# Layer 2 of a graph attention network: columns 256 to 767 of half of a tile's rows summed on TensorE, the first norm's statistics on ScalarE

## The chip, the cores and the metric

The kernel runs on one core of one Trainium2 chip. The metric is device time in microseconds (us), the median of the runs. The core has five engines that run their own instruction streams in order and wait for each other by semaphores: TensorE (PE, with its weight loads as PEld), VectorE (DVE), ScalarE (ACT), GpSimd (POOL) and SyncE (SP, which here only starts transfers).

## The reference

Two graph attention layers over 10000 nodes and 170000 edges (80000 drawn in both directions and a loop on each node; the layer adds a loop of its own), all in float32:

```python
def gat_conv(x, edge_index, W, a_src, a_dst, bias, heads, out_ch, concat):
    src, dst = edge_index with self loops
    xl = (x @ W).reshape(n, heads, out_ch)
    e = leaky_relu(alpha_src[src] + alpha_dst[dst], 0.2)     # alpha_* = einsum of xl with a_*
    e = exp(e - segment_max(e, dst)[dst])
    alpha = e / (segment_sum(e, dst)[dst] + 1e-16)
    out = segment_sum(xl[src] * alpha, dst) + bias            # heads side by side, or their mean

h  = gat_conv(x, W1, heads=4, out_ch=256)                     # 1024 columns
h1 = relu(layer_norm(h, g1, be1)) + (x @ Wr1 + br1)
h  = gat_conv(h1, W2, heads=1, out_ch=768)                    # 768 columns
out = layernorm(x + layer_norm(h, g2, be2) + (h1 @ Wr2 + br2))
```

The change lies in the last two lines: for every node the weighted sum over its neighbours' rows of 768 numbers, the residual product h1 @ Wr2, the first norm (with g2 and be2) and the second one of the sum with x.

## The kernel before

The first part of the program sorts the nodes by degree into 79 tiles of 128 nodes and makes lists of their neighbours; then comes layer 1, and at its end a table in DRAM holds for each node its row of layer 2: 768 numbers of h1 @ W2, and two logits. Layer 2 (the function `ordered_layer2`) goes over the tiles one after the other. A tile has n rows, n being the largest number of neighbours in it (7 to 41; 17.35 on the mean, 1371 in all). Row k holds the k-th neighbour of each of the 128 nodes, one node on a partition, so that a row is 128 x 770 numbers. Row 0 (the node itself) is loaded by SP, the other 1292 rows come by an indirect DMA each, which POOL issues (`gather`, L473). They go into a ring of 41 places in SBUF: the gather for a row may start once all readers of the row that stood 41 places earlier are done, and POOL issues the gathers in the order of the rows, so a place that comes free late holds up all gathers behind it.

The work of a tile t is spread over two turns of the loop `for t in range(NT)`:

- In turn t-1, at row `turn`, `weights_of(t)` computes the logits of all rows of t (`logits`, L536 to L544: a few small instructions of DVE, and Exp on ACT), for which all gathers of tile t must have landed. Three rows later (`turn + LEAD`) `normalised` divides by their sum, and then `summed` lets ACT write a diagonal matrix of the weights e of each row (L1310) and PE multiply it with columns 512 to 767 of the row (L1311, in fp32 two matmul instructions each). These products of n - n//6 rows add up in PSUM, on the bank that holds the residual's last 256 columns (`big`), together with the bias b2 (L1320).
- At the top of turn t-1 stands `residual(t)`, 16 products of h1 with Wr2 (L1363, 32 instructions), so PE's order is residual, sums, residual, sums.
- In turn t, DVE adds e times the first 512 columns of each row to `acc` in PSUM (`weigh`, L574), and for the last n//6 rows also the columns 512 to 767 onto PE's sums (L1439). At row n//2 SP loads the operand of `residual(t + 2)` (512 KB) and x of the next tile (384 KB).
- After the last row come the statistics of the first norm (L585, L587 on DVE, L589 and L590 on ACT). The rest of the norms follows in turn t+1: at row 3 (LEAD) the first norm and the two additions (L599, L601, L1373, L1374 on DVE), at row 6 the second norm on ACT (L1378 to L1384), at row 9 the scatter of the finished 128 rows to the output on POOL (L1386).

Tiles of 26 rows and more (three of the 79, the last one among them) are parted: their logits and sums are made in two parts, and a factor `fade` brings the first to the second one's maximum. The order in which each engine gets its instructions is the order of this code, written by hand (`manual_schedule`). In the views, `w` are pieces of the old weight buffer w2 that now hold h1, x, the tile being normed and some of the diagonals; `big` is a PSUM tile of two banks.

## Time and profile before

| what | us |
| --- | --- |
| median of 3 runs (lowest to highest) | 5207.22 (5200.71 to 5215.73) |
| the profiled execution | 5214.41 |
| its span | 5212.5 |
| layer 2, first gather to last gather | 3174.05 to 5159.25 |
| PE, DVE, ACT, POOL busy over the span | 4580.7, 4359.7, 3210.2, 3481.6 |
| granted TensorE clock over the span | 0.931 |

The views are of the profiled execution; times are us from the start of the span unless ns is written. In a row of a group, the count is followed by the busy time, the mean ns of one instruction, and the idle time of the engine just before them with what ended it. "issue" is time in which an engine waited for nothing that the profile shows. "remote" is a release that the profile puts down to none of the engines shown. Matmuls are pipelined, so the mean of one is longer than its share of the busy time. A row of the timeline is start, duration, engine, line and what ran, and in brackets the idle time before it.

### The profile page before, as it was taken

The numbers are of one execution on the slowest core, as the hardware profiler recorded it, in microseconds if no ns is written. First come the engines' busy times: TensorE is split into PE (matmuls) and PEld (weight loads), VectorE is DVE, ScalarE is ACT, GpSimd is POOL, SyncE is SP. The second block draws the span as 40 slices with busy tenths as digits, with TensorE's granted clock in tenths as the row PEclk, the third lists the DMA queues.
The fourth block names the chain that finished last, engine by engine and source line by source line (L and its number), as shares of the span: only waits on it lengthen the run. The fifth ranks groups of instructions, "written<-read, shape, count | busy, mean of one in ns | idle before, by whom it ended". The sixth has DMA issues, their size and how long they took to land. (4 is left out here: it accounts for less than half of the span.)

```text
span 5212.5 us, 56646 instructions
## 1 busy us (share of the span) xinstructions
PE 4580.7 (88%) x13332; PEld 2524.8 (48%) x13332; DVE 4359.7 (84%) x7113; ACT 3210.2 (62%) x9002; POOL 3481.6 (67%) x3722
## 2 busy tenths in 40 slices
PE   9999997999999997899999997877887877788876
PEld 4443444554444443444445554554554555555554
DVE  7887877999998988888999985888787878888877
ACT  5744446899998987898999982433333333333333
POOL 6876756666776766676766644767667666666664
PEclk9999998999999998999999998988888888888888
DMA  4333449999999989999999977999899999999995
GB/s 154 122 107 125 109 150 346 347 364 370 381 381 377 382 299 329 346 374 370 375 379 370 359 266 265 333 323 328 312 323 326 329 326 324 325 324 326 323 326 194
DMA packets 433436, 1588.28 MB, mean 305 GB/s; under 512 B 77208, under 2 KB 82136, under 8 KB 433095
## 3 DMA queue, kind: packets, MB, share of 16 engines
q0 software_dynamic: 321040, 1283.72, 68.1%
q1 hardware_dynamic: 99490, 269.38, 14.3%
q10 hardware_dynamic: 12564, 31.47, 1.9%
q8 instruction: 112, 1.84, 0.1%
q14 instruction: 230, 1.88, 0.1%
HBM read 1426.26 MB, written 177.29 MB: 308 GB/s over the span
## 5 line engine op out<-in xcount | busy, mean ns | idle before, releaser
L473 POOL DMA_INDIRECT ring<-table,slots x2663 | 2677.3, 1005 | 1366.0 <-issue 588.7
L563 ACT ACTIVATE ring<-ring,e 128x256 f32<-128x256 f32 x4468 | 1823.9, 502 | 65.3 <-DVE e L981 38.6
L574 DVE SCALAR_TENSOR_TENSOR acc<-ring,e,acc 128x512 f32<-128x512 f32 (+1 forms) x2280 | 1456.9, 639 | 97.4 <-PE acc L936 21.2
L570 DVE TENSOR_TENSOR acc<-acc,ring 128x1024 f32<-128x1024 f32 x869 | 1070.1, 1231 | 81.2 <-ACT ring L563 16.9
L1363 PE MATMUL big<-wr,w 128*128 128x512 f32 (+1 forms) x2464 | 834.9, 495 | 46.2 <-issue 46.0
L1161 PE MATMUL half<-w,hT 128*128 128x512 f32 (+1 forms) x2528 | 843.5, 486 | 4.0 <-issue 3.7
L180 PE MATMUL big<-wr,xT 128*128 128x512 f32 x1896 | 833.9, 596 | 0.5 <-ACT xT L897 0.5
L1311 PE MATMUL big<-ring,diagonals 128*128 128x256 f32 x1706 | 527.7, 449 | 298.6 <-issue 264.1
L1363 PEld LDWEIGHTS big<-wr,w 128*128 128x128 f32 x2464 | 478.6, 194 | 391.8 <-issue 357.7
L1161 PEld LDWEIGHTS half<-w,hT 128*128 128x128 f32 x2528 | 472.5, 189 | 348.4 <-issue 310.3
L1311 PEld LDWEIGHTS big<-ring,diagonals 128*128 128x128 f32 x1706 | 383.9, 227 | 427.4 <-issue 338.3
L180 PEld LDWEIGHTS big<-wr,xT 128*128 128x128 f32 x1896 | 357.2, 192 | 420.8 <-issue 420.0
L936 PE MATMUL acc<-ring,ident 128*128 128x512 f32 x992 | 467.8, 621 | 86.8 <-ACT ring L563 61.3
L544 ACT ACTIVATE e<-e 128x19 f32<-128x19 f32 (+14 forms) x82 | 17.6, 215 | 641.6 <-issue 243.1
L695 ACT ACTIVATE scr<-scr 128x256 f32<-128x256 f32 x624 | 250.5, 403 | 160.6 <-DVE scr L688 153.6
L936 PEld LDWEIGHTS acc<-ring,ident 128*128 128x128 f32 x992 | 190.9, 197 | 326.1 <-issue 195.9
L635 PE MATMUL one<-wr,mixed 128*128 128x512 f32 x702 | 307.6, 592 | 0.0
L1310 ACT ACTIVATE diagonals<-ident,e 128x128 f32<-128x128 f32 x853 | 259.1, 387 | 70.7 <-DVE total L552 20.3
L589 ACT ACTIVATE sd<-mv,eps 128x1 f32<-128x1 f32 x158 | 46.1, 292 | 400.1 <-issue 159.9
L1311 PE MATMUL big<-ring,w 128*128 128x256 f32 x672 | 199.1, 436 | 65.9 <-issue 56.5
L700 POOL TENSOR_TENSOR row<-row,none 128x1024 f32<-128x1024 f32 x69 | 168.2, 2438 | 116.0 <-DVE scr L688 45.1
L635 PE MATMUL one<-w,xT 128*128 128x512 f32 x492 | 228.5, 602 | 9.3 <-DMA w<-in_W_dram 6.4
(246 smaller groups left out, 4809.6 us busy)
## 6 DMA issues: line engine op xcount, KB each, us to landing
ring<-table,slots POOLq DMA_INDIRECT x2663
h_d<-hT SPq DMA_DIRECT2D x79, 512.0 KB
table<-row SPq DMA_DIRECT2D x78, 516.0 KB
w<-h_d SPq DMA_DIRECT2D x77, 512.0 KB
table<-row SPq DMA_DIRECT2D x79, 385.0 KB
ring<-table SPq DMA_DIRECT2D x79, 385.0 KB
w<-x_d SPq DMA_DIRECT2D x79, 384.0 KB
x_d<-xt SPq DMA_DIRECT2D x77, 384.0 KB
```

The source lines that it names most:

```text
L180: nc.tensor.matmul(p[:, c:e], aT[:, j, :], w[:, j, c:e], start=(j == 0), stop=(j == k - 1))
L473: nc.gpsimd.indirect_dma_start(out=to, out_offset=None, in_=table, in_offset=bass.IndirectOffsetOnAxis(ap=index, axis=0), **more)
L563: nc.scalar.activation(row[:, s], row[:, s], AF.Copy, scale=e[:, h:h + 1])
L570: nc.vector.tensor_add(acc[:, :c], acc[:, :c], row[:, :c])
L574: nc.vector.scalar_tensor_tensor(acc[:, s], row[:, s], e[:, h:h + 1], (acc if first is None else first)[:, s], op0=OP.mult, op1=OP.add)
L635: nc.tensor.matmul(p, aT[:, j, :], w[:, j, :], start=(start and j == 0), stop=(j == k - 1), skip_group_check=True)
L695: nc.scalar.activation(m[:, s], m[:, s], AF.Copy, accum_out=row[:, C1 + i * H1 + h:C1 + i * H1 + h + 1])
L936: nc.tensor.matmul(acc[:, c:c + BANK], ident, ring.slot(q + k)[:, c:c + BANK], start=(k == 0), stop=(k == m - 1))
L1161: nc.tensor.matmul(q, hT[:, j, :], w2[:, j, c:c + q.shape[1]], start=(j == 0), stop=(j == K1 - 1))
L1310: nc.scalar.activation(diagonal, ident, AF.Copy, scale=e[:, k - lo, :])
L1311: nc.tensor.matmul(to, diagonal, ring.slot(at + k)[:, ON_PE2:C2], start=False, stop=(k == n - 1 - by_vector(t)), skip_group_check=True)
L1363: nc.tensor.matmul(r[:, c:d], hT[:, j, :], wr2[:, j, c:d], start=(j == 0), stop=(j == K1 - 1 and d < C2), skip_group_check=True)
```

## The change

The split of the sums is turned. For the first half of a tile's rows (`on_pe`; of the first part, where a tile is parted) PE now sums columns 256 to 767 in products of 512 into two PSUM tiles of its own (`accs`), and DVE adds columns 0 to 255 of these rows beside them; for the other half DVE adds all 768 columns on top of PE's sums, and PE has no part in them. ACT instead of PE puts b2 into the accumulator (from the third tile on). ACT copies each residual out of PSUM into SBUF (`held`). The sum and the squares of the first norm are taken on ACT, as they already are in the second norm. The second stage of `norms` comes at row `soon` = min(6, n // 2, n - 4) instead of row 3, behind the logits of the next tile in most turns. Four rows of the second part of each parted tile are summed whole on PE, and the steps of that part come earlier. There are 16 diagonals instead of 28.

```diff
--- before.py
+++ after.py
@@ -50,9 +50,8 @@
 RING1 = 31
 RING2 = 41
 LEAD = 3
-DIAGONALS = 20
-ON_PE2 = 512
-ALL_BY_VECTOR = 6
+DIAGONALS = 8
+ALONE2 = 256
 SHARE = 4
 ON_PE1 = 5
 PARTED2 = 26
@@ -1239,7 +1238,7 @@
         at = [FIRST1[t] + k for t in turns for k in range(SLOTS1[t])]
         with tc.tile_pool(name="b2", bufs=1) as pool, tc.tile_pool(name="small2", bufs=2) as small, \
                 tc.tile_pool(name="ps_acc2", bufs=2, space=PSUM) as ps_acc, \
-                tc.tile_pool(name="ps_q2", bufs=3, space=PSUM) as ps_big, tc.manual_schedule():
+                tc.tile_pool(name="ps_q2", bufs=2, space=PSUM) as ps_big, tc.manual_schedule():
 
...
@@ -1282,19 +1281,16 @@
                 n = SLOTS[t]
                 return [0, n - 8 if t == NT - 1 else n // 2, n] if n >= PARTED2 else [0, n]
 
...
+            def on_pe(t):
+
+                return cuts_of(t)[1] // 2
 
             def parted_at(t):
 
                 lo = cuts_of(t)[1]
-                return ((LEAD + 1, 2 * LEAD + 1) if whole(t) else (lo - LEAD, lo - 1)) if len(cuts_of(t)) > 2 else ()
+                if len(cuts_of(t)) == 2:
+                    return ()
+                return (LEAD + 1, 2 * LEAD + 1) if t == NT - 1 else (lo - 3 * LEAD, lo - 2 * LEAD)
 
             def weights_of(t):
 
@@ -1302,33 +1298,38 @@
                 n, at, cuts = SLOTS[t], FIRST[t], cuts_of(t)
                 ad = small.tile([P, H2], F32, name="ad")
                 nc.vector.tensor_add(ad, ring.slot(at)[:, C2:C2 + H2], lift)
-                to = rs[t][:, C2:2 * C2 - ON_PE2]
-
-                def summed(e, lo, hi, more=None, m=0):
-                    for k in range(lo, hi):
-                        diagonal = next(turning)
-                        nc.scalar.activation(diagonal, ident, AF.Copy, scale=e[:, k - lo, :])
-                        nc.tensor.matmul(to, diagonal, ring.slot(at + k)[:, ON_PE2:C2],
-                                         start=False, stop=(k == n - 1 - by_vector(t)), skip_group_check=True)
-                        if k - lo < m:
-                            nc.tensor.matmul(more, diagonal, ring.slot(at + k)[:, :ON_PE2],
-                                             start=False, stop=(k - lo == m - 1), skip_group_check=True)
-                        if k - lo == m - 1:
-                            nc.scalar.copy(ring.slot(at + lo)[:, :ON_PE2], more)
-
-                def add_b2():
-                    nc.tensor.matmul(to, ident, b2_b[:, ON_PE2:], start=False, stop=False, skip_group_check=True)
+
+                def diagonal_of(e):
+                    diagonal = next(turning)
+                    nc.scalar.activation(diagonal, ident, AF.Copy, scale=e)
+                    return diagonal
+
+                def multiplied(to, a, row, lo, hi, start, stop):
+                    for c in range(lo, hi, BANK):
+                        d = min(hi, c + BANK)
+                        nc.tensor.matmul(to[:, c - lo:d - lo], a, row[:, c:d], start=start, stop=stop,
+                                         skip_group_check=True)
 
                 e, top = logits(small, ring, at, at + cuts[1], ad, H2, C2)
                 yield {0: (e, None, None)}
+                accs[t] = ps_acc.tile([P, 2 * BANK], F32, name="acc")
+                to, m = accs[t][:, BANK:], on_pe(t)
                 if len(cuts) == 2:
                     normalised(small, e, H2, turns[t])
-                    add_b2()
+                    if t < 2:
+                        multiplied(to, ident, b2_b, ALONE2, C2, True, False)
+                    else:
+                        nc.scalar.copy(to, b2_b[:, ALONE2:])
                 else:
                     doubled(e, turns[t])
                     total = small.tile([P, H2], F32, name="total")
                     nc.vector.reduce_sum(total, e.rearrange("p k h -> p h k"), axis=AX.X)
-                summed(e, 0, cuts[1] - by_vector(t))
+                for k in range(m):
+                    multiplied(to, diagonal_of(e[:, k, :]), ring.slot(at + k), ALONE2, C2,
+                               not k and len(cuts) > 2, k == m - 1)
+                held = pool.tile([P, C2], F32, name="held", bufs=2)
+                nc.scalar.copy(held, rs.pop(t)[:, :C2])
+                rs[t] = held
...
-                    nc.scalar.activation(to, to, AF.Copy, scale=fade)
-                    add_b2()
-                    m, more = whole(t), b2_b[:, :ON_PE2]
-                    if m:
-                        more = ps_big.tile([P, 2 * BANK], F32, name="big")[:, :ON_PE2]
-                        nc.tensor.matmul(more, ident, b2_b[:, :ON_PE2], start=True, stop=False, skip_group_check=True)
-                    summed(e, lo, hi, more, m)
-                    yield lo, (e, fade, ring.slot(at + lo)[:, :ON_PE2] if m else more)
+                    more = ps_big.tile([P, 2 * BANK], F32, name="big")
+                    multiplied(more, ident, b2_b, 0, C2, True, False)
+                    for k in range(WHOLE):
+                        multiplied(more, diagonal_of(e[:, k, :]), ring.slot(at + lo + k), 0, C2, False, k == WHOLE - 1)
+                    nc.scalar.copy(ring.slot(at + lo)[:, :C2], more[:, :C2])
+                    yield lo, (e, fade, ring.slot(at + lo)[:, :C2])
 
             def residual(t):
 
@@ -1360,26 +1359,30 @@
                 for c in range(0, C2, BANK):
...
-            def norms(t, h, r, means):
-
-                stats = deviation(small, [a for m in means for a in pieces(m, C2 - ON_PE2)])
+            def mean_and_deviation(spare, a):
+
+                less, inv = (small.tile([P, 1], F32, name=n, bufs=4) for n in ("less", "inv"))
+                nc.scalar.activation(spare, a, AF.Copy, accum_out=less)
+                nc.scalar.activation(less, less, AF.Copy, scale=-1.0 / C2)
+                nc.scalar.activation(spare, a, AF.Square, bias=less, accum_out=inv)
+                nc.scalar.activation(inv, inv, AF.Ln, scale=1.0 / C2, bias=eps)
+                nc.scalar.activation(inv, inv, AF.Exp, scale=-0.5)
+                return less, inv
+
+            def norms(t, h, r, sums):
+
+                less, inv = mean_and_deviation(h, sums)
                 yield
-                scaled(h, means, stats, g2_b, be2_b)
-                nc.vector.tensor_add(h, h, r[:, :C2])
+                nc.vector.scalar_tensor_tensor(h, sums, less, g2_b, op0=OP.add, op1=OP.mult)
+                nc.vector.scalar_tensor_tensor(h, h, inv, be2_b, op0=OP.mult, op1=OP.add)
+                nc.vector.tensor_add(h, h, r)
                 nc.vector.tensor_add(h, h, xs.pop(t))
                 yield
                 o = pool.tile([P, C2], F32, name="out")
-                less, inv = (small.tile([P, 1], F32, name=n) for n in ("less", "inv"))
-                nc.scalar.activation(o, h, AF.Copy, accum_out=less)
-                nc.scalar.activation(less, less, AF.Copy, scale=-1.0 / C2)
-                nc.scalar.activation(o, h, AF.Square, bias=less, accum_out=inv)
-                nc.scalar.activation(inv, inv, AF.Ln, scale=1.0 / C2, bias=eps)
-                nc.scalar.activation(inv, inv, AF.Exp, scale=-0.5)
+                less, inv = mean_and_deviation(o, h)
                 nc.scalar.activation(less, less, AF.Copy, scale=inv)
                 nc.scalar.activation(o, h, AF.Identity, bias=less, scale=inv)
                 yield
@@ -1387,12 +1390,15 @@
                     out=out, out_offset=bass.IndirectOffsetOnAxis(ap=nodes(turns[t]), axis=0),
                     in_=o, in_offset=None, bounds_check=N - 1, oob_is_err=False)
 
...
@@ -1405,39 +1411,36 @@
                     ahead = weights_of(t)
                     ready += itertools.islice(ahead, 2)
                 es, later, cuts = dict(ready[0]), ahead, cuts_of(t)
-                acc = ps_acc.tile([P, BANK], F32, name="acc")
+                sums = accs.pop(t)[:, ALONE2:]
                 if not t:
                     ring.fetch(RING2)
                 next(last, None)
+                soon = min(2 * LEAD, n // 2, n - LEAD - 1)
                 ready, ahead, turn = [], iter(()), n
                 if t + 1 < NT:
 
                     ahead = weights_of(t + 1)
                     turn = min(max(n // 3, cuts[-2] + 1, n + cuts_of(t + 1)[1] + 4 * LEAD - ring.size), n - LEAD)
...
                 for k in range(n):
                     if k in parted_at(t):
                         es.update([e for e in [next(later)] if e])
                     if k in (turn, turn + LEAD):
                         ready += itertools.islice(ahead, 1)
-                    if k in (LEAD, 2 * LEAD, 3 * LEAD):
+                    if k in (soon, soon + LEAD, soon + 2 * LEAD):
                         next(last, None)
                     lo = max(c for c in cuts[:-1] if c <= k)
                     weights, fade, more = es[lo]
                     row = ring.slot(FIRST[t] + k)
                     if k == 0 and len(cuts) > 2:
-                        nc.vector.tensor_scalar(acc[:, :ON_PE2], row[:, :ON_PE2], weights[:, 0], None, op0=OP.mult)
-                    else:
-                        if k == lo and fade is not None:
-                            nc.vector.scalar_tensor_tensor(acc[:, :ON_PE2], acc[:, :ON_PE2], fade, more,
-                                                           op0=OP.mult, op1=OP.add)
-                        if not lo or k - lo >= whole(t):
-                            weigh(acc, row, weights[:, k - lo], ON_PE2, None if k else b2_b)
-                            if k >= n - by_vector(t):
-                                sums = rs[t][:, C2:2 * C2 - ON_PE2]
-                                nc.vector.scalar_tensor_tensor(sums, row[:, ON_PE2:C2], weights[:, k - lo], sums,
-                                                               op0=OP.mult, op1=OP.add)
+                        nc.vector.tensor_scalar(sums[:, :ALONE2], row[:, :ALONE2], weights[:, 0], None, op0=OP.mult)
+                    elif k < on_pe(t):
+                        weigh(sums, row, weights[:, k], ALONE2, None if k else b2_b)
+                    elif lo and k == lo:
+                        nc.vector.scalar_tensor_tensor(sums, sums, fade, more, op0=OP.mult, op1=OP.add)
+                    elif not lo or k - lo >= WHOLE:
+                        weigh(sums, row, weights[:, k - lo], C2)
                     ring.fetch(FIRST[t] + k + 1 + ring.size)
                     if k == n // 2:
                         if t + 2 < NT:
@@ -1449,8 +1452,8 @@
                     pass
                 if not t:
                     nc.vector.tensor_add(be2_b, be2_b, adds[1])
-                    nc.vector.tensor_add(be2_b, be2_b, q[:, :C2])
-                last = norms(t, h, rs[t], [acc, rs[t][:, C2:2 * C2 - ON_PE2]])
+                    nc.vector.tensor_add(be2_b, be2_b, br2_q)
+                last = norms(t, h, rs.pop(t), sums)
             for _ in last:
                 pass
```

DVE, at the end of a tile of 17 rows and the start of the next one, before (`acc` with `e` are the sums, `mv` the statistics, `norm_90` is g2):

```order
L574 SCALAR_TENSOR_TENSOR acc<-ring,e,acc 128x512 x7
L1439 SCALAR_TENSOR_TENSOR big<-ring,e,big 128x256
L574 SCALAR_TENSOR_TENSOR acc<-ring,e,acc 128x512
L1439 SCALAR_TENSOR_TENSOR big<-ring,e,big 128x256
L585 BN_STATS st<-acc 128x6 x2
L585 BN_STATS st<-big 128x6
L587 BN_AGGR mv<-st 128x2
L574 SCALAR_TENSOR_TENSOR acc<-ring,e,b_22696 128x512
L574 SCALAR_TENSOR_TENSOR acc<-ring,e,acc 128x512 x2
L599 SCALAR_TENSOR_TENSOR w_88<-acc,mv,norm_90 128x512
```

and of the change:

```order
L573 SCALAR_TENSOR_TENSOR acc<-ring,e,acc 128x768 x9
L573 SCALAR_TENSOR_TENSOR acc<-ring,e,b_22696 128x256
L573 SCALAR_TENSOR_TENSOR acc<-ring,e,acc 128x256 x4
L1300 TENSOR_TENSOR ad<-ring,lift 128x1
L535 TENSOR_TENSOR e<-ring,ad 128x13
L196 SCALAR_TENSOR_TENSOR e<-e 128x13
L539 TENSOR_REDUCE new<-e 128x1
L542 TENSOR_TENSOR e<-e,new 128x13
L573 SCALAR_TENSOR_TENSOR acc<-ring,e,acc 128x256
L1379 SCALAR_TENSOR_TENSOR w_88<-acc,less,norm_90 128x768
```

DVE's first reading of PE's sums moved from the last two rows of the tile to the ninth of 17, the statistics left its stream, and the norm moved behind the next tile's logits (L535 to L542).

PE, a residual, the sums of one tile and the next residual, before:

```order
L1363 MATMUL big<-wr_89,w_88 128x512 x8
L1363 MATMUL big<-wr_89,w_88 128x256 x8
L1320 MATMUL big<-b_22696,ident 128x256
L1311 MATMUL big<-ring,diagonals 128x256 x12
L1311 MATMUL big<-ring,w_88 128x256 x3
L1363 MATMUL big<-wr_89,w_88 128x512 x8
```

and of the change:

```order
L1362 MATMUL big<-wr_89,w_88 128x512 x8
L1362 MATMUL big<-wr_89,w_88 128x256 x8
L1310 MATMUL acc<-ring,diagonals 128x512 x7
L1310 MATMUL acc<-ring,w_88 128x512
L1362 MATMUL big<-wr_89,w_88 128x512 x8
```

The place of the sums between two residuals is the same; 15 products of 256 columns and the one for b2 became 8 of 512 columns.

ACT, of the change, around the copy of a residual (`w_88` with `acc` are the first norm's statistics, `out` is the second norm):

```order
L1322 COPY acc<-b_22696 128x512
L1304 ACTIVATE w_88<-ident,e 128x128 x3
L1304 ACTIVATE diagonals<-ident,e 128x128 x6
L1331 COPY held<-big 128x768
L1368 ACTIVATE out,less<-w_88 128x768
```

The copy of the residual that PE computes after these sums stands ahead of the second norm in ACT's stream.

16 lines of the change are left out of this document (6 added, 10 removed).

## The prediction

> **What bounds the kernel now.** Only layer 2 changes, so I read it alone. First the busy times by stretch (us, then the mean granted clock, the share of time in which the DMA engines were busy, and GB/s): layer 2, its end, and 50 us of layer 1 for comparison.
>
> ```profile
> core 0: us, PE busy (x) PEld busy (x) DVE busy (x) ACT busy (x) POOL busy (x), PEclk, DMA share, GB/s
> 3174.00:5160.00 1986.00, 1563.38 (x4983) 1035.53 (x4982) 1587.07 (x3064) 701.91 (x2108) 1366.39 (x1369) 0.86 0.92 324
> 1550.00:1600.00 50.00, 49.37 (x146) 25.53 (x145) 43.90 (x65) 44.39 (x114) 34.82 (x44) 1.00 1.00 376
> ```
>
> No engine is full in layer 2, and the transfers come near it: 0.92 of the time at 324 GB/s, where layer 1 got 376. So something keeps gathers from being asked for. The groups of POOL and PE and their waits in layer 2 say what:
>
> ```profile
> L473 POOL DMA_INDIRECT ring<-table,slots x1292 | 1279.1, 990 | 658.1 <-issue 285.8 <-PE big L1311 116.8 <-remote 105.9
> L1386 POOL DMA_INDIRECT out_dram<-out,order x79 | 89.5, 1133 | 64.0 <-POOLq L1674 22.5 <-issue 19.8 <-ACT out L1384 18.0
> POOL ring L473 <- issue: 285.8, 926, 2.0
> POOL ring L473 <- PE big L1311: 116.8, 98, 5.2
> POOL ring L473 <- remote: 105.9, 51, 4.1
> PE big L1311 <- issue: 320.6, 247, 11.2
> ```
>
> A gather holds POOL for 0.99 us, and 285.8 / 926 = 0.31 us of issue follow. POOL without any stall would need 1292 x (0.990 + 0.30) + 79 x (1.133 + 0.30) = 1780 us. It takes 1986: **206 us of stalls**, and 116.8 + 105.9 of idle time before gathers were ended by PE's products L1311 and by a release without a name. PE itself waits for nearly nothing in these products except "issue". One tile of 17 rows shows both sides (start, duration, what ran; PE, then POOL, then DVE):
>
> ```profile
> 4927.86 0.59 PE L1320 MATMUL big<-b,ident 128*128 128x256 f32 x2
> 4928.30 2.97 PE L1311 MATMUL big<-ring,diagonals 128*128 128x256 f32 x13
> 4935.45 0.59 PE L1311 MATMUL big<-ring,diagonals 128*128 128x256 f32 x2 [1.53 <-issue]
> 4937.57 1.50 PE L1311 MATMUL big<-ring,diagonals 128*128 128x256 f32 x2 [1.54 <-issue]
> 4940.69 2.74 PE L1311 MATMUL big<-ring,w 128*128 128x256 f32 x6
> 4943.25 10.50 PE L1363 MATMUL big<-wr,w 128*128 128x512 f32 x32
> 4954.02 2.32 PE L1311 MATMUL big<-ring,w 128*128 128x256 f32 x10
> 4936.76 0.95 POOL L473 DMA_INDIRECT ring<-table,slots  x1 [0.30 <-issue]
> 4940.13 0.95 POOL L473 DMA_INDIRECT ring<-table,slots  x1 [2.42 <-PE big L1311]
> 4934.09 0.18 DVE L536 TENSOR_TENSOR e<-ring,ad 128x17 f32<-128x17 f32 x1 [4.49 <-DMA ring<-table,slots]
> 4934.82 2.33 DVE L574 SCALAR_TENSOR_TENSOR acc<-ring,e,acc 128x512 f32<-128x512 f32 x3
> 4937.99 6.29 DVE L574 SCALAR_TENSOR_TENSOR acc<-ring,e,acc 128x512 f32<-128x512 f32 x8
> 4944.39 0.49 DVE L1439 SCALAR_TENSOR_TENSOR big<-ring,e,big 128x256 f32<-128x256 f32 x1
> ```
>
> PE goes from sums to residual to sums without a pause for data: 4928.30 to 4954.02 is 25.7 us, one tile. Thirteen instructions run in 2.97 us, then for some 9 us they trickle, one or two at a time, with gaps of 0.5 to 1.5 us that nothing in the profile explains, and run at speed again at the end. While they trickle POOL stalls once, 2.42 us in place of 0.30, on a product that has not run, and once in a tile DVE waits, here 4.49 us, for the last row of the next tile to land. So a tile's period is set by a chain: products trickle, ring places come free late, gathers start late. DVE, 1587 of 1986 us busy, has its waits at the end of this chain.
>
> **The change part by part.**
>
> *DVE.* The groups, with rows of ScalarE's work for the parts below:
>
> ```profile
> L574 DVE SCALAR_TENSOR_TENSOR acc<-ring,e,acc 128x512 f32<-128x512 f32 x1288 | 971.4, 754 | 40.4 <-DVE acc L574 2.9 <-issue 2.6 <-remote 1.6
> L1439 DVE SCALAR_TENSOR_TENSOR big<-ring,e,big 128x256 f32<-128x256 f32 x182 | 88.2, 485 | 107.7 <-PE big L1311 49.9 <-remote 41.9 <-issue 14.7
> L601 DVE SCALAR_TENSOR_TENSOR w<-w,sd,norm 128x768 f32<-128x768 f32 x79 | 80.6, 1020 | 21.9 <-ACT sd L590 7.0 <-remote 5.5 <-DVE w L599 1.1
> L1373 DVE TENSOR_TENSOR w<-w,big 128x768 f32<-128x768 f32 x79 | 75.3, 954 | 3.2 <-issue 0.3 <-DVE w L601 0.3
> L1378 ACT ACTIVATE out<-w 128x768 f32<-128x768 f32 x79 | 65.7, 832 | 154.5 <-DMA out_dram<-out,order 58.9 <-DVE w L1374 34.7 <-issue 32.3
> L1380 ACT ACTIVATE out<-w,less 128x768 f32<-128x768 f32 x79 | 73.9, 935 | 2.6
> L1384 ACT ACTIVATE out<-w,less,inv 128x768 f32<-128x768 f32 x79 | 81.1, 1027 | 3.7 <-ACT less L1383 1.1
> L1310 ACT ACTIVATE diagonals<-ident,e 128x128 f32<-128x128 f32 x853 | 259.1, 387 | 70.7 <-DVE total L552 20.3 <-PE big L1311 13.7 <-DVE e L554 11.1
> ```
>
> Before, its sums are 1367 rows x 0.754 + 182 x 0.485 = 1119 us. After, 645 rows go at 256 columns, 0.485 us each, and 717 at 768 columns. That length on PSUM is not in the trace: by the slope of the two rows it is 0.754 + 0.269 = 1.02 us, and L601 (SBUF alone) has 1.02, L1373 0.95. So 313 + 731 = 1044 us, 75 less (125 less with 0.95). Statistics leave it, and the first step of the norm is one instruction instead of two. All of this is worth nothing by itself: DVE's period has 4.49 us of waiting in the tile above, and its work would only wait longer.
>
> *ACT* gains two passes over 768 columns for the statistics (0.83 and 0.94 us, as L1378 and L1380), the residual's copy and b2's copy (768 and 512 wide: between nothing and 0.83 us each), and loses about 7 diagonals of 0.387 = 2.7 us: nearly even, and 702 of 1986 us busy covers it.
>
> *PE* has now 2378 instructions in the sums, and 158 for b2. After, 645 products of 512 and 12 whole rows in the parted tiles, with a few for b2, are some 1354 instructions: 0.534 of 2536. For their time:
>
> ```profile
> L1363 PE MATMUL big<-wr,w 128*128 128x512 f32 x1232 | 559.5, 605 | 16.0 <-issue 15.8
> L1311 PE MATMUL big<-ring,diagonals 128*128 128x256 f32 x1706 | 527.7, 449 | 298.6 <-issue 264.1 <-DMA ring<-table,slots 7.3 <-ACT diagonals L1310 4.8
> L1311 PE MATMUL big<-ring,w 128*128 128x256 f32 x672 | 199.1, 436 | 65.9 <-issue 56.5 <-remote 3.7 <-DMA ring<-table,slots 2.4
> ```
>
> Busy, the sums take 727 us, 0.306 each. A product of 512 columns takes 559.5 / 1232 = 0.454 in the residual, so 1354 take 615 us, and up to 800 if they run as slowly in the trickle as the narrow ones do there: between 112 less and 80 more. The gaps are the larger question. If a gap belongs to an instruction, 320.6 us become 171 (149 less). If it belongs to anything else, none goes.
>
> *The sum.* I take the gaps by instruction, since the trickle is a row of single instructions with a gap before each; but I let the end be set by POOL, which is the last of the chain. Its stall goes down with the instructions that it waits for: 206 x 0.534 = 110, **96 us less**. PE's own account (149 less in gaps, between 112 less and 80 more in work) gives 69 to 261 less, with POOL's 206 as the most that can show; 96 lies at the careful end, because a shorter row of products still ends after POOL has begun to stall. At the end of the program one wait goes, the last of PE's products before the statistics:
>
> ```profile
> 5159.25 0.95 POOL L473 DMA_INDIRECT ring<-table,slots  x1 [0.31 <-issue]
> 5164.98 0.43 DVE L585 BATCH_NORM_STATS2 st<-big 128x6 f32<-128x256 f32 x1 [5.85 <-PE big L1311]
> ```
>
> 5.85 us, less about 0.7 for statistics in a chain of ACT instead of DVE and 1.6 for the wider last rows: 4 us less. The profiled execution took 5214 us, 7 more than the median of the runs; 5214 - 96 - 4 = 5114 there, and **5107 us** as a median.
>
> *Moved steps.* The norm goes behind the logits: it then stands between them and row n/2. The scatter goes back three rows on POOL; a gather behind it is held 1.13 us, as now. PE's sums must be whole at row n/2 instead of at the last n//6 rows, which the third rival prices. The copy `held` waits on ACT for the whole residual: for the next tile that ends at 4943.25 + 10.50 = 4953.75, and behind it are queued the second norm (passes of 0.83, 0.94 and 1.03 us, by estimate 4 us with the short instructions between them) and the statistics (0.83 and 0.94, some 3 us), which are then ready at about 4961.5. DVE wants them one period after 4934.82 + 0.5, at 4961, or a microsecond earlier with the forecast's shorter period. That is half a microsecond to two, inside DVE's waits.
>
> **The rivals.** *The stall vanishes.* With half the products the row ends before POOL comes to the ring place; then 5207 - 206 - 4 = 4997. For it: PE's account reaches that far. Against: transfers, which are at 0.92 already. At 1986 x 0.92 = 1827 us the share would be 1.00, which gives 5207 - 159 - 4 = 5044, unless their rate rises to layer 1's.
>
> *Nothing moves.* The trickle is the transfers' own: PE's instructions come slowly while gathers fill the queues, for as long as these are full, and whether 15 or 8 products stand in the row is the same. Then only the end's 4 us go: 5203. For it: gaps of about one gather's spacing (0.5 to 1.5 us against 1.25). Against it: a shorter row simply has fewer instructions to be late.
>
> The Trainium skill ("Runtime: NRT & Kernel Launch", section "Instruction fetch mechanics") says that an engine's instruction store is refilled in blocks by a DMA queue of its sequencer while the engine executes, and that this cost is mostly hidden. By that rule no gap belongs to an instruction's supply, and the result would be this rival's; the row of 320.6 us of issue does not agree that PE is always supplied.
>
> *Slower.* DVE needs all of PE's sums at row n/2. In the tile above DVE after the change would do row 5, the norm (1.02 + 1.02 + 0.95 + 0.96 = 3.95), rows 6 and 7 and the division of the weights (0.93, from 4937.06 to 4937.99) from 4934.8 on: 0.49 + 3.95 + 0.97 + 0.93 = 6.3, so row 8 stands at 4941.2. PE's row of products began at 4928.30 and ended at 4943.25. If the eight wide products take as long as the fifteen narrow ones do now, DVE waits 2.05 us, with nine wide rows (9.2 us) still to come and their ring places held as long. The point is a row of products of 12.9 us from its start. DVE waits already 43 times at L1439:
>
> ```profile
> DVE big L1439 <- PE big L1311: 49.9, 27, 6.5
> DVE big L1439 <- remote: 41.9, 10, 11.8
> DVE big L1439 <- issue: 14.7, 6, 8.6
> ```
>
> 43 x 2.05 = 88 us more: 5295, with all tiles 5365, with 20 of them 5248. Against it: half the instructions must take over 86% of the present time.
>
> **How the numbers follow.** Forecast 0.45, stall gone 0.15, nothing moves 0.17, slower 0.23. Differences under 0.3% (16 us) cannot be told from none, so faster 0.60, same 0.17, slower 0.23. The forecast's own range is 5054 (149 us less of gaps, all of it seen) to 5155 (the stall goes down only with all of PE's instructions per tile, 64 to 49, which is 48 us). The 8 in 10 range reaches below to 4990, just past the stall gone, and above to 5275, through half of the slower case; about 1 in 10 is left out on either side.
>
> **What would show it.** In the changed profile: idle time of POOL before gathers ended by PE's products near 110 us over the 1292 x 0.30 of issue; PE's issue gaps in the sums near 170 us; the logits' wait for the last landing kept, or longer; DVE at row n/2 hardly waiting for PE; DMA share about 0.96. Wrong: gaps of PE still over 300 us with half the instructions (nothing moves), or a wait at row n/2 of over 1 us a tile (slower), or POOL at 1.29 us a gather throughout (stall gone).

## The result, and the profile after

The changed kernel took 5370.92 us (median, 5363.65 to 5375.01), the kernel before 5203.97 beside it: 1.0312 of it, with an interval of 1.0297 to 1.0327. It is slower by 167 us; 5107 us had been forecast, with a range up to 5275.

In the profiled execution of the changed kernel (5361.8 us of span) the gathers of layer 2 go from 3161.61 to 5301.47, 2139.9 us, where they took 1985.2 before: 155 us more. The end behind the last gather is 7 us longer, and layer 2 happened to start 12 us earlier. So the loss lies in the loop over the tiles. Its busy times (columns as before):

```profile
core 0: us, PE busy (x) PEld busy (x) DVE busy (x) ACT busy (x) POOL busy (x), PEclk, DMA share, GB/s
3174.00:5313.00 2139.00, 1581.63 (x3820) 779.54 (x3819) 1440.57 (x2485) 811.50 (x2130) 1369.63 (x1359) 0.86 0.85 300
```

VectorE works 147 us less than before, and the transfers stand still more: 0.85 of the time busy, not 0.92. The groups of the changed kernel in layer 2 that answer to those of before:

```profile
L472 POOL DMA_INDIRECT ring<-table,slots x1292 | 1300.3, 1006 | 551.4 <-issue 323.7 <-DVE acc L573 99.2 <-DMA table<-row 62.3
L1389 POOL DMA_INDIRECT out_dram<-out,order x79 | 80.9, 1024 | 320.0 <-ACT out L1387 290.3 <-issue 14.3 <-POOLq L1677 13.0
L573 DVE SCALAR_TENSOR_TENSOR acc<-ring,e,acc 128x768 f32<-128x768 f32 x714 | 729.8, 1022 | 37.7 <-issue 10.1 <-DVE acc L573 6.6
L573 DVE SCALAR_TENSOR_TENSOR acc<-ring,e,acc 128x256 f32<-128x256 f32 x566 | 276.4, 488 | 18.3 <-issue 2.2
L573 DVE SCALAR_TENSOR_TENSOR acc<-ring,e,b 128x256 f32<-128x256 f32 x76 | 37.4, 492 | 427.8 <-PE acc L1310 291.8 <-PE big L1362 67.3 <-remote 53.4
L1310 PE MATMUL acc<-ring,diagonals 128*128 128x512 f32 x646 | 381.3, 735 | 250.3 <-issue 119.0 <-ACT diagonals L1304 100.2 <-ACT out L1387 12.2
L1310 PE MATMUL acc<-ring,w 128*128 128x512 f32 x644 | 372.7, 724 | 257.9 <-issue 178.9 <-ACT w L1304 47.1 <-ACT acc L1322 14.2
L1331 ACT COPY held<-big 128x768 f32<-128x768 f32 x79 | 62.0, 785 | 321.2 <-remote 180.5 <-PE acc L1310 116.9 <-PE big L1362 23.8
```

Three of these waits are new or nearly so. The fifth row is row 0 of each tile on VectorE (the row that starts from b2, `b`): VectorE stands idle 428 us ahead of it, 5.4 us a tile, and TensorE's products end 292 us of that; before, it did not wait there at all. The last row is ScalarE's copy of the residual: 321 us of waiting ahead of it. And POOL waits 290 us for ScalarE's second norm before it can issue the scatter, where it waited 18. TensorE's products wait for their diagonals, 100 and 47 us, which they never did before (4.8 us and less), and the gaps without a cause are 298 us where they were 321, though the instructions are 1290 where they were 2378. By the same sum as before, POOL's own pace is 1292 x 1.306 + 79 x 1.324 = 1792 us, and its stalls are 2140 - 1792 = 348 us instead of 206.

One tile from the timeline shows how the new waits hang together (PE, then ScalarE, then VectorE):

```profile
4917.49 4.46 PE L1310 MATMUL acc<-ring,diagonals 128*128 128x512 f32 x10
4921.78 10.48 PE L1362 MATMUL big<-wr,w 128*128 128x512 f32 x32
4940.04 3.63 PE L1310 MATMUL acc<-ring,diagonals 128*128 128x512 f32 x4 [7.78 <-issue]
4948.69 6.99 PE L1310 MATMUL acc<-ring,w 128*128 128x512 f32 x10 [1.26 <-issue]
4955.52 10.48 PE L1362 MATMUL big<-wr,w 128*128 128x512 f32 x32
4939.59 0.99 ACT L1304 ACTIVATE diagonals<-ident,e 128x128 f32<-128x128 f32 x3 [4.91 <-DVE e L553]
4949.03 0.80 ACT L1331 COPY held<-big 128x768 f32<-128x768 f32 x1 [7.00 <-remote]
4929.10 0.49 DVE L573 SCALAR_TENSOR_TENSOR acc<-ring,e,b 128x256 f32<-128x256 f32 x1 [11.16 <-PE big L1362]
4939.35 0.18 DVE L553 TENSOR_TENSOR e<-e,total 128x17 f32<-128x17 f32 x1
4955.72 0.49 DVE L573 SCALAR_TENSOR_TENSOR acc<-ring,e,b 128x256 f32<-128x256 f32 x1 [4.58 <-PE acc L1310]
```

Row 0 of the second tile starts at 4955.72, when that tile's last product ends (4948.69 + 6.99 = 4955.68), and not eight rows later. From row 0 of a tile to the next tile's weights VectorE needs 4929.10 to 4939.35 and their own 0.18, 10.4 us; only then can ScalarE write the diagonals (4939.59) and PE begin the next products (4940.04), 7.8 us after its residual had ended at 4932.26. Products, row 0, weights, products: a ring of waits, here 26.6 us around. And in the first tile row 0 came at 4929.10, although PE's record has the last product end at 4921.95. The residual ended at 4932.26 by the same record; ScalarE was free for its copy from about 4942.0, and the copy came at 4949.03. So by these records TensorE's releases arrive late in the stretches where its instructions trickle.

### The profile page after: what moved, and what is told of

Same layout as the page of the kernel before. It is cut to its first block, busy times and chain, and to the rows that moved or that the text cites. A ratio compares the mean times of both kernels' runs of the same rounds, so it can differ in the third digit from the quotient of the medians.

```text
span 5361.8 us, 52991 instructions
## 1 busy us (share of the span) xinstructions
PE 4590.8 (86%) x12140; PEld 2260.9 (42%) x12140; DVE 4213.9 (79%) x6528; ACT 3317.5 (62%) x9018; POOL 3493.4 (65%) x3722
## 5 line engine op out<-in xcount | busy, mean ns | idle before, releaser
L573 DVE SCALAR_TENSOR_TENSOR acc<-ring,e,acc 128x256 f32<-128x256 f32 (+1 forms) x2272 | 1491.8, 657 | 111.7 <-PE acc L935 22.2
L1310 PE MATMUL acc<-ring,diagonals 128*128 128x512 f32 x646 | 381.3, 735 | 250.3 <-issue 119.0
L1310 PE MATMUL acc<-ring,w 128*128 128x512 f32 x644 | 372.7, 724 | 257.9 <-issue 178.9
L573 DVE SCALAR_TENSOR_TENSOR acc<-ring,e,b 128x256 f32<-128x256 f32 x76 | 37.4, 492 | 427.8 <-PE acc L1310 291.8
L1310 PEld LDWEIGHTS acc<-ring,diagonals 128*128 128x128 f32 x646 | 147.9, 235 | 464.8 <-issue 311.0
L1310 PEld LDWEIGHTS acc<-ring,w 128*128 128x128 f32 x644 | 144.9, 233 | 460.3 <-issue 366.9
L1389 POOL DMA_INDIRECT out_dram<-out,order x79 | 80.9, 1024 | 320.0 <-ACT out L1387 290.3
L1331 ACT COPY held<-big 128x768 f32<-128x768 f32 x79 | 62.0, 785 | 321.2 <-remote 180.5
```

What stands on the lines that cost most here:

```text
L573: nc.vector.scalar_tensor_tensor(acc[:, s], row[:, s], e[:, h:h + 1], (acc if first is None else first)[:, s], op0=OP.mult, op1=OP.add)
L1310: nc.tensor.matmul(to[:, c - lo:d - lo], a, row[:, c:d], start=start, stop=stop, skip_group_check=True)
L1389: nc.gpsimd.indirect_dma_start(out=out, out_offset=bass.IndirectOffsetOnAxis(ap=nodes(turns[t]), axis=0), in_=o, in_offset=None, bounds_ch ...
```

## The experiments

The sets of runs are of two kinds, and each ratio below is to the kernel before in the same set. In three sets the kernel before took 5204, 5205 and 5269 us ("first kind"), in three others 4963, 4961 and 4960 ("second kind"). The expectations speak of chips of the first and the second kind, but what sets them apart, two chips or one in two conditions, isn't shown. The record gives the chip the same number, 8, in the set of 5269 us and in that of 4961, so the kinds need not be two chips. In the traces of the second kind TensorE's gaps without a cause are missing (below).

**1. Row 0 without TensorE's sums.** The edit, on the changed kernel:

```diff
 ...
-weigh(sums, row, weights[:, k], ALONE2, None if k else b2_b)
+nc.vector.scalar_tensor_tensor(sums[:, :ALONE2] if k == on_pe(t) - 1 else side, row[:, :ALONE2],
+                               weights[:, k], side if k else b2_b[:, :ALONE2], op0=OP.mult, op1=OP.add)
```

> The changed kernel, but VectorE's columns 0 to 255 of the first half of the rows add up in a buffer of their own in SBUF, and only the last of these rows writes into the accumulator that TensorE also writes; so VectorE meets TensorE's sums first at row n/2 - 1 and not at row 0. Theory 1 (the first row of a tile waits on VectorE for the last of TensorE's products, and VectorE's way from that row to the next tile's weights, some 10.9 us, is then in a ring with these products): the 428 us of waiting at row 0 go, the ring shrinks to some 3 us beside the products, and a tile's time is TensorE's 10.5 us of residual and 8.7 to 15 us of sums, 22.5 (POOL's own) to 25.5 us: 5010 to 5245 us in all. Theory 2 (the time is lost in ScalarE's order: the copy of the residual holds up the second norm, and that holds up the scatter on POOL and so all gathers, 257 us): the wait at row 0 is a symptom, and the time stays above 5300 us.

First kind: 5328.1 us, 1.0235 (1.0218 to 1.0252). The wait at row 0 is gone, and 99 us stand at the row that writes into the accumulator; but the time fell by 43 us only. That is far from theory 1's range and in theory 2's (above 5300 us). Where the waiting went (VectorE's groups of this run):

```profile
L1379 DVE SCALAR_TENSOR_TENSOR w<-acc,less,norm 128x768 f32<-128x768 f32 x79 | 80.1, 1015 | 231.3 <-ACT w L1370 225.9 <-issue 5.4
L1440 DVE SCALAR_TENSOR_TENSOR acc<-ring,e,side 128x256 f32<-128x256 f32 x79 | 38.9, 492 | 99.4 <-remote 62.9 <-PE big L1362 24.5 <-issue 6.5
```

The norm now waits 226 us for ScalarE's statistics, which stand in ScalarE's stream behind the copy of the residual and the second norm. In the changed kernel this wait was 30 us, hidden by the one at row 0. So there is a second ring of waits: residual, copy, statistics, norm on VectorE, weights, products and the next residual.

**2. The scatter later.** The third step of the norms at the end of the turn instead of at row soon + 6:

```diff
-if k in (soon, soon + LEAD, soon + 2 * LEAD):
+if k in (soon, soon + LEAD):
```

> The changed kernel with the scatter of the finished rows issued at the end of a tile's turn instead of at row soon + 6, so that POOL reaches it when ScalarE's second norm is long done. Theory 1: POOL's 257 us of waiting before the scatter go elsewhere, and the time stays at 5371 us within 16. Theory 2: they are what was lost, and the time falls to 5115 to 5250 us.

First kind: 5379.62 us, 1.0332 (1.0315 to 1.0349), as the change itself. That is in theory 1's range. But POOL still waited 241 us for the second norm there (257 in the change, both without the very last scatter), so the edit did not take the wait away, and this run alone does not tell the theories apart.

**3. The copy of the residual later.** Behind the statistics instead of behind the diagonals, in tiles that are not parted:

```diff
-held = pool.tile([P, C2], F32, name="held", bufs=2)
-nc.scalar.copy(held, rs.pop(t)[:, :C2])
-rs[t] = held
+if len(cuts) > 2:
+    rs[t] = kept(rs.pop(t))
 ...
 less, inv = mean_and_deviation(h, sums)
+if len(cuts_of(t)) == 2:
+    r = kept(r)
 yield
```

`kept` makes the same copy.

> The changed kernel with the copy of the residual out of PSUM moved on ScalarE from behind the next tile's diagonals to behind the first norm's statistics (in tiles that are not parted), so that it no longer stands ahead of the second norm and waits for TensorE there. Theory 1: the row-0 ring does not hold this copy; the time stays at 5371 us within 30. Theory 2: the second norm and the scatter come in time, 5115 to 5250 us.

First kind: 5334.53 us, 1.0242 (1.0225 to 1.0259). Neither range was met: POOL's wait before the scatter fell from 257 us to 85, counted as in run 2, and the copy waits for nothing, and yet only 36 us came of it. The mirror image of run 1, in two groups of this run:

```profile
L573 DVE SCALAR_TENSOR_TENSOR acc<-ring,e,b 128x256 f32<-128x256 f32 x76 | 37.5, 493 | 517.8 <-PE acc L1310 201.9 <-remote 193.8 <-PE big L1361 109.9
L1367 ACT COPY held<-big 128x768 f32<-128x768 f32 x79 | 61.6, 780 | 0.0
```

Row 0 now waits 518 us where it waited 428. Neither theory stands alone: where one wait is taken out, the other grows.

**4. The wait at row 0 in the kernel before.** One small instruction and nothing else of the change:

```diff
+if k == 0:
+    nc.vector.tensor_copy(small.tile([P, 1], F32, name="seen"), rs[t][:, C2:C2 + 1])
```

> The kernel before, with one instruction more on VectorE: at row 0 of each tile it copies one column of TensorE's sums of that tile (128 x 1, about 0.15 us), which makes row 0 wait for the last of these products, as in the changed kernel. Nothing else of the change is in it. Theory 1: row 0 to the next tile's weights is then some 13 us (the norm's 5.7, five rows, the logits), which with 15.5 us of products makes 28.5 us a tile where there were 25.3: 5204 + 79 x 3.2 = about 5450 us, at least 5350. Theory 2: the wait at row 0 costs nothing by itself, 5204 + 12 = 5216 us, at most 5260.

First kind: 5507.95 us, 1.0576 (1.0558 to 1.0593), 303 us more. Who VectorE waited for at the new instruction (us, times, longest):

```profile
DVE seen L1430 <- PE big L1363: 223.2, 30, 10.1
DVE seen L1430 <- remote: 186.1, 23, 10.6
DVE seen L1430 <- PE big L1311: 158.4, 25, 17.2
```

The wait at row 0 costs by itself what theory 1 says, at least 5350 us. That it costs more here than in the change is put down, without a run of its own, to the longer ring: 15 products and rows 512 columns wide stand in it.

**5. Both rings opened**, the edits of 1 and 3 together, in a set of each kind, with the change and the kernel before unedited beside the second:

> The changed kernel with both edits of the first runs at once: columns 0 to 255 of the first rows in a buffer of their own, and the copy of the residual behind the statistics on ScalarE. With the first edit alone VectorE waited 224 us for ScalarE's statistics, which stood behind the copy; so each edit alone left the other ring. If these two rings are what the change lost, the time falls to that of the kernel before or under it, 5050 to 5210 us. If the change loses elsewhere (its wide products, the norm behind the logits), it stays above 5290 us, near the 5328 and 5335 us of the single edits.

> The changed kernel with both rings opened, again. If the rings are what the change lost on either kind of chip, it is within 0.5% of the kernel before, or under it, on a chip of the first kind too (5050 to 5230 us), as it was on the second (1.001). If on the first kind the late signals of TensorE cost the change something beyond the rings, it stays 2% and more above, over 5300 us.

> The changed kernel unedited, beside the two below on one chip, since the kernel before took 5205 us on the chip of the first runs and 4963 us on that of the second, where no gaps of TensorE's products without a cause appear in any trace. On a chip of the first kind: 5371 us within 16. On one of the second kind: if the rings cost by themselves, 100 us and more above the kernel before (1.02 and more); if they cost only through TensorE's late signals, within 0.5% of it.

> The kernel before, for its trace on the same chip. On a chip of the first kind some 320 us of gaps of TensorE's products, as in the first trace; on one of the second kind under 50 us, and POOL's stalls (time of the gathers beyond 1.29 us each) near nothing.

First kind: both opened 5253.21 us, 0.9973 (0.9962 to 0.9985), beside the change's 5430.68, 1.0303 (1.0285 to 1.0321). Second kind: 1.0013 (1.0003 to 1.0023). The times expected for the first kind were missed, as the kernel before took 65 us more in this set than in the first, and the ratios came as expected. So the two edits, which alone brought 43 and 36 us, bring 177 together (in another set; 3.3% of the kernel before, where the change lost 3.0%): they give back all that the change lost. On the first kind they leave a gain of 15 us, on the second a loss of 6. These busy times and groups are of both opened, then of the kernel before, in that first-kind set:

```profile
3180.00:5208.00 2028.00, 1599.96 (x3927) 789.98 (x3925) 1453.37 (x2505) 811.94 (x2131) 1352.80 (x1369) 0.88 0.90 320
L1361 PE MATMUL big<-wr,w 128*128 128x512 f32 x1232 | 675.9, 690 | 285.7 <-issue 207.5 <-ACT held L1367 38.9 <-ACT inv L1376 19.8
L1310 PE MATMUL acc<-ring,w 128*128 128x512 f32 x644 | 312.7, 622 | 66.1 <-issue 37.2 <-ACT w L1304 18.3 <-DMA ring<-table,slots 4.7
L1310 PE MATMUL acc<-ring,diagonals 128*128 128x512 f32 x646 | 307.5, 622 | 55.4 <-ACT diagonals L1304 26.4 <-issue 19.1 <-DMA ring<-table,slots 10.0
```

```profile
3180.00:5212.00 2032.00, 1587.07 (x5067) 1056.88 (x5066) 1598.93 (x3077) 706.46 (x2118) 1361.61 (x1369) 0.85 0.90 319
L1363 PE MATMUL big<-wr,w 128*128 128x512 f32 x1232 | 552.6, 601 | 11.9 <-issue 11.0 <-PE big L1311 0.8
L1311 PE MATMUL big<-ring,diagonals 128*128 128x256 f32 x1706 | 533.8, 458 | 304.2 <-issue 260.9 <-DMA ring<-table,slots 20.3 <-ACT diagonals L1310 3.5
L1311 PE MATMUL big<-ring,w 128*128 128x256 f32 x672 | 195.3, 435 | 68.9 <-issue 59.6 <-DMA ring<-table,slots 4.2 <-ACT diagonals L1310 2.4
```

The gaps without a cause have left the sums (56 us in place of 320), and stand in the residual, which had 11 and now has 208: whatever PE runs in the slow stretch trickles. POOL's stalls stay: 2028 - 1352.8 - 1369 x 0.30 = 264 us with both opened, 2032 - 1361.6 - 1369 x 0.30 = 260 us before.

**6. The change where the gaps are missing.** Unedited, with the kernel before beside it:

> The changed kernel unedited. On a chip of the first kind 1.030. On one of the second kind, where it has not run yet: with the plain write the changed kernel stood 2.1% above the kernel before with the same edit there (4982 and 4880 us) without any late signals, so the rings cost by themselves, and the changed kernel is 1.015 to 1.03 of the kernel before; if the scatter's time on POOL covers part of them, 1.005 to 1.015.

> The kernel before, for its trace on the same chip. On a chip of the second kind: gaps of TensorE's products without a cause under 50 us, and POOL's time beyond 1.29 us a gather and 1.43 us a scatter under 60 us.

Second kind: the change 5042.52 us, 1.0165 (1.0148 to 1.0182); the kernel before 4960. Busy times and TensorE's groups of the kernel before there:

```profile
3180.00:4908.00 1728.00, 1408.09 (x4845) 976.24 (x4844) 1551.37 (x2990) 684.80 (x2056) 1322.84 (x1320) 0.91 0.97 359
L1311 PE MATMUL big<-ring,diagonals 128*128 128x256 f32 x1676 | 442.1, 423 | 198.2 <-ACT diagonals L1310 185.3 <-DMA ring<-table,slots 12.9
L1363 PE MATMUL big<-wr,w 128*128 128x256 f32 x1216 | 274.9, 379 | 0.0
```

No gap of the sums is left that has no cause, with the same instructions as on the first kind (layer 2 begins earlier here, at 3116, so these views leave out its first gathers and sums and their counts are smaller). POOL's stalls are 1728 - 1322.8 - 1320 x 0.30 = 9 us: it is at its own pace, and little is left there for the change to win. Of the change there:

```profile
3180.00:4989.00 1809.00, 1467.99 (x3701) 742.60 (x3700) 1412.27 (x2423) 793.85 (x2086) 1334.25 (x1321) 0.89 0.94 343
L573 DVE SCALAR_TENSOR_TENSOR acc<-ring,e,b 128x256 f32<-128x256 f32 x74 | 36.3, 491 | 202.6 <-PE acc L1310 202.5
L1310 PE MATMUL acc<-ring,w 128*128 128x512 f32 x644 | 360.7, 713 | 197.6 <-ACT w L1304 190.8 <-DMA ring<-table,slots 6.8
L1331 ACT COPY held<-big 128x768 f32<-128x768 f32 x77 | 59.7, 775 | 0.0
```

Row 0 still waits 203 us for products, and products wait 191 us (and 120 in the other group) for diagonals: the first ring alone, with no late release in it; the copy waits for nothing. It is the wait at row 0 that tells the two kernels apart: the kernel before has none there, though its products too wait 267 us for diagonals (185 and 82). POOL's stalls are 1809 - 1334.25 - 1321 x 0.30 = 78 us where they were 9, and the change costs 82 us. No run here opens the first ring alone. On the first kind, where the releases come late and the copy waits too, it is 162 to 167.

**7. A plain write in place of the scatter.** In the kernel before, in the change, and in the change with both rings opened; SP writes the tile's rows as they stand, so the order of the nodes in the output is left out:

```diff
-nc.gpsimd.indirect_dma_start(out=out, out_offset=bass.IndirectOffsetOnAxis(ap=nodes(turns[t]), axis=0), ...)
+first = turns[t] * P
+nc.sync.dma_start(out[first:min(first + P, N), :], o[:min(P, N - first), :])
```

> The kernel before, with the finished rows written by SP as they stand in the tile (one plain transfer of the same 384 KB) and not by POOL's indirect scatter: the order of the nodes in the output is left out. In the trace of before each scatter's 64 packets are followed at once by some 12 us in which gather packets take over 0.4 us where they took 0.2, the rate falls from 400 to 300 GB/s, and TensorE's products trickle, until the gathers have drained. Theory S (the scatter among the gathers brings on this slow stretch, and the slow stretch is POOL's 206 us and TensorE's 320 us of gaps): the slow stretches go, gaps of TensorE's products under 100 us, 4990 to 5060 us. Rival (they come from the gathers themselves, and the scatter only stands ahead of them): gaps still 250 to 330 us, and the time falls by at most the 79 x 1.43 us that POOL no longer spends, 5090 to 5205 us.

> The changed kernel with the same plain write in place of the scatter (the order of the nodes in the output is left out). If the rings through VectorE's row 0 and ScalarE's copy cost only because TensorE's signals come late in the slow stretches, they close in under POOL's 22.5 us a tile without them (10.9 us + 8 of products): 4990 to 5080 us, within 1% of the kernel before with the same edit. If the rings cost by themselves, it stays at least 100 us above that one.

> The kernel before with the plain write by SP in place of POOL's scatter (the order of the nodes in the output is left out), again, hoped to fall on a chip of the first kind (kernel before 5200 to 5270 us), where TensorE's products have gaps without a cause. There, theory S (the scatter brings on the slow stretches): gaps of TensorE's products under 100 us, and 0.955 to 0.970 of the kernel before. Rival (the gathers do it alone): gaps 250 to 330 us, and 0.98 to 1.00. On a chip of the second kind: 0.983 as before, and it says nothing on this.

> The changed kernel with both rings opened and the same plain write. Theory S: as the run above within 0.5%, since the rings are open and the slow stretches gone. Rival: 0.98 to 0.995 of the kernel before, TensorE's gaps (sums and residual) 200 to 300 us.

All of these, and a third run of the first, fell on the second kind, so the theory on the scatter was not tested. The kernel before goes to 0.9834, 0.9847 and 0.9855, which is 72 to 83 us of the 79 x 1.36 = 107 us (1.06 of scatter and 0.30 of issue) that POOL no longer spends. The change with this write is 1.0037 (1.0025 to 1.0050), 102 us above the kernel before with it; with both rings opened it is 0.9821 (0.9801 to 0.9840), level with it. That is the rings once more, with no scatter at all: 102 us is just within what was expected if they cost by themselves (at least 100).

**8. The scatters of two tiles together**, in the kernel before, with two output buffers and 22 diagonals instead of 28:

> The kernel before, with the scatters of two tiles issued together after every second tile (two output buffers instead of one, 22 diagonals instead of 28): the same work, but 40 places of scatter among the gathers instead of 79. Theory S: about half of the slow stretches go, 206 us of stall become some 110 to 140, 5105 to 5150 us, and the gaps of TensorE's products fall from 320 to 160 to 220 us. Rival: as before within 16 us, 5188 to 5220 us.

Second kind: 5184.43 us, 1.0437 (1.0420 to 1.0454). A clear loss that neither theory expected. TensorE waited 465 us for diagonals and VectorE 310 for landings (267 and 94 in the kernel before on this kind); whether the pair of scatters among the gathers or the fewer diagonals did it was not tried apart.

**9. The other two parts of the change**, each put back with both rings opened: the statistics on VectorE (`deviation(small, pieces(sums, ALONE2))`), and the norm at row 3 (`soon = LEAD`).

> The changed kernel with both rings opened and the first norm's statistics back on VectorE (three instructions of 0.42 us and one of 0.24, 118 us in all). If that part of the change is worth nothing by itself, as VectorE's waits cover it: 0.997 of the kernel before within 0.4%. If VectorE's work now sets the pace: up to 118 us more, 1.01 to 1.02.

> The changed kernel with both rings opened and the first norm's scaling back at row 3, ahead of the next tile's logits, where VectorE waits for the last landing. If the place behind the logits costs (4 us of norm between the logits and the next weights): 0.97 to 0.99 of the kernel before. If those 4 us are hidden in either place: 0.997 within 0.4%. If it waits there for ScalarE's statistics, as the tile's end is only three rows before: 1.00 to 1.01.

Second kind: 1.0014 (1.0004 to 1.0024) and 0.9994 (0.9984 to 1.0005), beside 1.0013 for both opened alone. These runs show no difference between the engines for the statistics, and some 0.2% for the place of the norm, between two sets.

No version was shown to beat the kernel before on both kinds: both rings opened gain 0.3% on the first kind and lose 0.1% on the second.

## Why the prediction was wrong

- **The step that failed: "PE's sums must be whole at row n/2".** They must be whole at row 0, where VectorE stood idle for 428 us. Columns 0 to 255 of VectorE and columns 256 to 767 of TensorE lie in one accumulator tile, and row 0 writes into it, so VectorE waits there for the last of TensorE's products. The third rival had the mechanism and the sign, but its place is eight rows too late, and its price (2.05 us in 43 tiles, 88 us) took only VectorE's own delay. At row 0 the wait closes a ring with the next tile's weights, which come 10.4 us behind it. Run 1 removes it, run 4 makes it in the kernel before (303 us), and runs 6 and 7 show it alone, at 82 and 102 us. (The rival's own sums differ by 4 us: 5295 and 5248 leave out the gain at the end, 5365 has it in.)
- **The copy `held`: half a microsecond to two, "inside DVE's waits".** The prediction read the order of ScalarE's queue rightly (the code has PE compute this residual ahead of the tile's sums, not after them as the text ahead of the prediction says), and it took the residual to release the copy when it ends. In the tile above the copy came 17 us after the recorded end. The copy waits 321 us in all, and with row 0 free VectorE waits 226 us behind it (run 1). Priced from the lengths of the instructions alone, the step left out that the release comes late in just the stretch that the prediction had described.
- **"I take the gaps by instruction".** Forecast: 171 us of gaps for 0.534 of the instructions, and POOL's stall down from 206 to 110 us. Measured: 298 us of gaps in the sums, and 348 us of stall. With the rings opened the gaps moved to the residual, 264 us in the sums and the wide residual where these had 332 (270 and 392 with the residual's narrow part and b2), and POOL's stall stayed at 264 us (260 before). That the gaps fell in part does not help: POOL's stall does not go with them. And on the second kind the same instructions have no such gaps. So the second rival was right on this step: the stretch is not the sums' own, and 8 products are late in it as 15 were. It is the forecast's 96 us that this takes away; the two rings of waits make the 167 us of loss.
- The Trainium skill ("Runtime: NRT & Kernel Launch", section "Instruction fetch mechanics") has it that filling an engine's instruction store is mostly hidden. The second kind agrees: 1676 and 672 instructions of the sums, and no gap without a cause. The first kind does not point at supply either: from 4887 to 4923 in the kernel before no packet moves on the queues that carry instructions, and one of the slow stretches, from 4908 to 4914, lies within. What the gaps are stays open.
- **VectorE's durations were right**: 1022 ns for the 768-wide row (1.02 us forecast), 1044 us of sums in all (1044). So was that its savings are worth nothing by themselves: 147 us less work, and the time rose. The place of the statistics makes no difference that run 9 shows, and that of the norm some 0.2%.
- **ScalarE "nearly even"** was 110 us too little: 812 us busy for 702, as the copies out of PSUM and into it (785 and 586 ns) and two passes on PSUM (800 and 900 ns, with 0.19 us each to read the sum) outweigh the diagonals. ScalarE had time enough for this; what cost was the place of the copy in its order.
- **The end**: 4 us less forecast, 7 us more measured. In the last tile VectorE still has twelve row sums behind the last weights (11.59 us), and then waits 2.23 us for the statistics.

## What to carry to other kernels

When two engines write different columns of one accumulator tile, look in the order of waits for the first instruction that touches the tile, not for the first that needs the other's result: give the early one a buffer of its own, or the slower engine's whole chain becomes a ring with the next tile. Two waits that cover each other show little when each is removed alone (43 and 36 us here, 177 together), so a small answer to one edit does not clear its cause. And a part that one engine hands to another is paid by where it stands in the other's queue, behind which release, more than by its length.

## What the runs showed of the hardware that was not expected

The same kernel took 5204 to 5269 us in some sets of runs and 4960 to 4963 in others, with the same instructions. Between the first trace of the kernel before and that of the second kind lie 254 us: 190 in the gathers of layer 2 (1985.2 and 1794.8 us), and 58 ahead of layer 2, which no run here explains. In layer 2 the first kind has slow stretches, in most tiles once: before one of them, inside it and after it, the kernel before (first kind) shows

```profile
4922.00:4928.00 6.00, 6.00 (x23) 4.15 (x23) 5.76 (x8) 0.27 (x2) 4.78 (x5) 1.00 1.01 405
4930.00:4940.00 10.00, 5.00 (x16) 2.78 (x15) 5.53 (x15) 4.87 (x13) 5.88 (x7) 0.82 0.87 296
4947.00:4953.00 6.00, 6.00 (x22) 3.86 (x21) 5.76 (x9) 0.50 (x2) 4.47 (x6) 1.00 1.00 393
```

The transfers fall from 405 to 296 GB/s, TensorE starts 16 matmul instructions in 10 us instead of 23 in 6, and what it releases arrives late, by 17 us in the changed kernel's tile above. Most packets of the gathers take as long there as elsewhere (0.235 us, the median); in the five stretches from 4853 to 4967 11% of them take over 0.4 us, and 4% outside, so the packets of over 0.4 us that the first text of run 7 speaks of are a few only. Between 4851 and 4956 the packets of five scatters pass, and each is followed within 4 us by such a stretch, which ends when the gathers have drained; another stretch, from 3316 to 3326, began 34 us after the last scatter. That the scatter brings it on was only argued, since the runs without it fell where the gaps are missing. It cannot be the scatter alone: on the second kind the same 79 scatters pass, and no such gap follows.
